# Token stage: small vector work moved to ScalarE, and the first convolution in three bf16 parts

## The chip, the cores and the metric

The kernel is one program on one core of a Trainium2 chip. The core has a matrix engine (TensorE, PE in the profile; its weight loads are PEld), VectorE (DVE), ScalarE (ACT), GpSimd (POOL) and SyncE (SP), which here issues the DMAs. Each engine takes its instructions in the order in which they stand in its own queue, and waits on semaphores for what other engines produce. The metric is the device time of one execution in microseconds (us).

## What is computed

Four layers follow one another on x of 64 images, 128 channels, 28 x 28 pixels, all in f32. Only the first and the last matter here.

Layer 0 is a residual block with quantised weights and activations:

```python
out = conv3x3(x, quant_weight(w1, 4))
out = quant_act(batchnorm(out, gamma1, beta1), 4)
out = conv3x3(out, quant_weight(w2 * (mask2 > 0.5), 4))
out = quant_act(batchnorm(out, gamma2, beta2) + x, 4)
```

`quant_weight` gives odd multiples of 1/15 between -1 and 1; the kernel keeps them as whole numbers from -15 to 15 and puts 1/15 into the scale of the batch norm. The input x of the first convolution is any f32 number.

Layer 1 is self-attention over the pixels of each image, layer 2 a Mamba scan over the pixels. Layer 3, the token stage, takes each pixel's 128 channels as a sequence of 8 tokens of 16 numbers and runs a Mamba over it, then normalises in four groups of channels and gates:

```python
xs = silu(causal_conv(xi)); dt, Bm, Cm = split(xs @ x_proj_w.T)
dt = softplus(dt @ dt_proj_w.T + dt_proj_b)
h = exp(dt * A) * h + dt * B * xs      # 8 tokens, 32 x 16 states a pixel
y = (sum over states of h * C) + xs * D
xr = (y * silu(z)) @ out_proj_w.T
gn = (xr - mu) * rsqrt(var + 1e-5)     # mean and variance of 32 channels and all pixels
out = x + silu(gn * gn_gamma + gn_beta)
```

## The kernel before

All tiles have 128 partitions. T is the 784 pixels of an image, and HT is half of that.

`conv_block` (L135) makes both convolutions. `quantised` (L147) prepares the weights: ScalarE takes the tanh, VectorE and one GpSimd reduction scale and round. The first weights q1 are f32 and the second, q2, are bf16. Then a loop over 32 pairs of images loads a pair into `xt` (128 x 2 x 784), and `conv3x3` (L116) makes each half image as nine matmuls, one per tap, that accumulate in PSUM; the source is a shifted window of the image and a tap at the border covers fewer columns. ScalarE copies the sum to `raw` (L182), VectorE takes the statistics (L184), and SyncE stores it. The pool of the large tiles holds three of each. After the batch norm (L101 to L112) a second loop reads `raw` back, quantises it with ScalarE (L196) and VectorE (L197, L199), and runs `conv3x3` on the bf16 tile `qa`.

`attention_and_mamba` (L491) records its operations in a plan of its own, which writes the order of the queues by its costs (all at L472 in the profile). The change does not touch it.

`token_mamba` (L1077) is a loop over 28 groups of 1792 pixels (14 columns of 128 pixels, G = 14), each in two halves of 16 of the 32 inner channels (dh = 0 and 1), each half in four blocks of four inner channels.

- `x_proj(k)` (L1179) makes B and C of a group: for each of seven pairs of pixel columns it loads rows, multiplies into a PSUM tile `two`, and copies that to `BC` (L1202), 512 columns that land in runs of two. It then makes the product of B and C summed over states (L1209 to L1216).
- `delta_u(k, dh)` (L1224) makes the step size and the input of a half: 16 `delta` scalings and four `u` copies on ScalarE, then softplus as max(v, 0) + log(1 + e) with e = exp(-abs(v)): two ScalarE steps, `w` = 1 + e on VectorE (L1254), two corrections on VectorE (L1255, L1256), the logarithm on ScalarE, and two GpSimd steps (L1259, L1260). L1263 makes `diag`.
- `exps(k, dh, i)` (L1266) is 64 exponentials of 98 columns on ScalarE that fill one `a` tile for one block. There are two such tiles.
- `block` (L1275) is the scan over the 8 tokens. GpSimd makes the inputs `db` (L1293, five tiles) and the first steps on `a` (L1304, L1306); VectorE multiplies, adds and reads out (L1305 to L1312) with the state h in PSUM; PE sums over the states with an identity (L1315, L1317, L1319) and so releases `a`; ScalarE copies the sum to `ysb`.
- `gate(k, dh, ysb)` (L1322) transposes back, multiplies (L1335, L1336) and, for dh = 1, projects (L1344) and copies the result to the image `xr` (L1354). When an image is full, `finish_image` (L1133) normalises and gates it: statistics on VectorE (L1137, L1139), the group mean by a matmul with `grp` (L1141), six one-column VectorE steps and two one-column ScalarE steps around a second group matmul (L1143 to L1152), two sign changes (L1153, L1154), three ScalarE steps for the gate's sigmoid, the scale and shift of the image on VectorE (L1162), and two GpSimd steps (L1164, L1165).

The results of `two`, the transposes and the group means take turns in one pool of three PSUM banks (`bank`). At the end of `token_mamba` generators mix the steps: while a half runs its blocks, it takes steps of the preceding half's `gate` (for dh = 1 they carry the images, so these run in the next half with dh = 0), of the next half's `delta_u`, and, in a dh = 0 half after its first block, of the next group's `x_proj`. From this program a scheduler with a simulated timeline then makes the order of each queue in the convolutions and the token stage. ScalarE operations of the token stage have the line of a helper, L228.

Of the kernel before, what the change touches and what calls it, by code (L numbers as in the profile page):

```python
# [16 lines left out]
F32 = mybir.dt.float32  # L17
BF16 = mybir.dt.bfloat16
# [7 lines left out]
C = 128  # L26
HW = 28
# [88 lines left out]
def conv3x3(nc, ps, w, src):  # L116

    img = src.rearrange("p (h w) -> p h w", w=HW)
    taps = [(0, 0)] + [(dy, dx) for dy in (-1, 0, 1) for dx in (-1, 0, 1) if (dy, dx) != (0, 0)]
    for half in range(2):  # L120
        acc = ps[:, half, :HT].rearrange("p (h w) -> p h w", w=HW)
        r0 = half * 14
        for i, (dy, dx) in enumerate(taps):
            lo, hi = max(r0, -dy), min(r0 + 14, HW - dy)
            a, b = max(0, -dx), min(HW, HW - dx)
            nc.tensor.matmul(  # L126
                acc[:, lo - r0 : hi - r0, a:b],
                lhsT=w[:, (dy + 1) * 3 + dx + 1, :],
                rhs=img[:, lo + dy : hi + dy, a + dx : b + dx],
                start=(i == 0),  # L130
                stop=(i == len(taps) - 1),
            )


def conv_block(tc, cpool, dram, x, w1t, w2t, m2t, v, eps):  # L135
# [6 lines left out]
    with ExitStack() as ctx:  # L142
# [4 lines left out]
        def quantised(name, src, mask, dtype):  # L147
# [19 lines left out]
            q = wp.tile([C, 9, C], dtype, name=f"q{name}")  # L167
# [3 lines left out]
        q1 = quantised("1", w1t, None, F32)  # L171
        q2 = quantised("2", w2t, m2t, BF16)

        st1 = wp.tile([C, NB * 2, 6], F32, name="st1")
        for g in range(NB // GRP):
            xt = big.tile([C, GRP, T], F32, name="xt")
            nc.sync.dma_start(xt, x[g * GRP : (g + 1) * GRP].rearrange("b c t -> c b t"))
            raw = big.tile([C, GRP, T], F32, name="raw")
            for k in range(GRP):
                acc = ps.tile([C, 2, 512], F32, name="acc")  # L180
                conv3x3(nc, acc, q1, xt[:, k, :])
                nc.scalar.copy(halves(raw[:, k, :]), acc[:, :, :HT])  # L182
                for h in range(2):
                    nc.vector.bn_stats(st1[:, (g * GRP + k) * 2 + h, :], raw[:, k, h * HT : (h + 1) * HT])  # L184
# [7 lines left out]
        for g in range(NB // GRP):  # L192
# [7 lines left out]
            for k in range(GRP):  # L200
                acc = ps.tile([C, 2, 512], F32, name="acc")
                conv3x3(nc, acc, q2, qa[:, k, :])
# [874 lines left out]
def token_mamba(tc, tables, x2d, utd, ztd, pk4, v, ident, eps, out, NB):  # L1077
# [17 lines left out]
    with ExitStack() as ctx:  # L1095
# [37 lines left out]
        def finish_image(b):  # L1133
# [8 lines left out]
            sm = p2.tile([C, 8], F32, name="sm", bufs=4)  # L1142
            nc.vector.tensor_copy(sm[:, 0:1], acc[:, 0:1])  # L1143
            nc.vector.tensor_sub(sm[:, 1:2], mv[:, 0:1], sm[:, 0:1])
            nc.vector.scalar_tensor_tensor(sm[:, 2:3], sm[:, 1:2], sm[:, 1:2], mv[:, 1:2], ALU.mult, ALU.add)
            acc2 = bank()
            nc.tensor.matmul(acc2[:, 0:1], lhsT=grp, rhs=sm[:, 2:3], start=True, stop=True)
            act(sm[:, 3:4], acc2[:, 0:1], AF.Ln, bias=eps)
            act(sm[:, 4:5], sm[:, 3:4], AF.Exp, scale=-0.5)
            nc.vector.tensor_mul(sm[:, 5:6], sm[:, 4:5], v("gn_gamma"))  # L1150
            nc.vector.tensor_mul(sm[:, 6:7], sm[:, 0:1], sm[:, 5:6])
            nc.vector.tensor_sub(sm[:, 7:8], v("gn_beta"), sm[:, 6:7])  # L1152
            nc.vector.tensor_scalar(sm[:, 0:1], sm[:, 5:6], -1.0, None, ALU.mult)  # L1153
            nc.vector.tensor_scalar(sm[:, 1:2], sm[:, 7:8], -1.0, None, ALU.mult)  # L1154
# [4 lines left out]
            act(e, xo, AF.Exp, bias=sm[:, 1:2], scale=sm[:, 0:1])  # L1159
            act(e, e, AF.Ln, bias=1.0)  # L1160
            act(e, e, AF.Exp, scale=-1.0)
            nc.vector.tensor_scalar(xo, xo, sm[:, 5:6], sm[:, 7:8], ALU.mult, ALU.add)  # L1162
# [16 lines left out]
        def x_proj(k):  # L1179
# [5 lines left out]
            for g, n in chunks:  # L1185
                uts = [load_rows(utd, k, dh, g, n) for dh in range(2)]
                for g2 in range(0, n, 2):
                    two = bank()
                    for j in range(2):
# [12 lines left out]
                    nc.vector.tensor_copy(  # L1202
                        BCf[:, :, g + g2 : g + g2 + 2], two.rearrange("p (c j) -> p c j", j=2)
                    )
# [19 lines left out]
        def delta_u(k, dh):  # L1224
# [29 lines left out]
            nc.vector.tensor_scalar(w_, e_, 1.0, None, ALU.add)  # L1254
# [244 lines left out]
```

## Time and profile before

| | us |
|---|---|
| median of 3 runs | 14449.58 (14403.58 to 14459.57) |
| profiled execution | 14456.75 |
| its span | 14454.9 |
| first convolution, first to last matmul | 18.6 to 744.6 |
| second convolution | 755.3 to about 940 |
| token stage, from its first preparation | 8085 |
| token stage, first to last block | 8144 to 14404, 6260 long |
| VectorE busy in these 6260 | 5781.8 |
| ScalarE | 4804.0 |
| GpSimd | 5165.3 |
| PE | 4363.2, mean clock 0.81 |

A group of instructions stands in the profile as line, engine, operation, output <- input, shapes and count; then busy time in us and the mean of one in ns; then the idle time of the engine just before these instructions and what ended most of it. A wait stands as engine, line and instruction that waits <- engine and line that it waited for, then total us, number of times, and the longest. Idle time of an engine that does not set the pace costs nothing.

### The profile page before, as it was taken

Reading aid. Unit: us, or ns where it says so; the run is one execution under the profiler, and the core shown is the slowest. Engines: PE = TensorE matmul, PEld = TensorE weight load, DVE = VectorE, ACT = ScalarE, POOL = GpSimd, SP = SyncE. Lnnn points to the kernel's source line nnn. Section 1 sums busy time; section 2 is a strip of 40 time slices with the busy share of each in tenths; the row PEclk is TensorE's granted clock in tenths of the full one; section 3 lists DMA queues with packets and bytes.
Section 4 is the critical chain, followed back from the end, with each engine's and each line's share of the span. In section 5 each row is a group of like instructions: output and inputs, shape, how many; then the busy total and the mean of one; then the engine's idle time right before and its main releaser. Section 6 shows DMA issues by size and latency. Waiting matters only on the chain. (4 is left out here: it accounts for less than half of the span.)

```text
span 14454.9 us, 181149 instructions
## 1 busy us (share of the span) xinstructions
PE 10855.2 (75%) x58370; PEld 7180.2 (50%) x58370; DVE 12706.4 (88%) x13524; ACT 10460.3 (72%) x25236; POOL 11391.7 (79%) x5304
## 2 busy tenths in 40 slices
PE   9987777777777777777776676776767767677676
PEld 5654444444444444444443455555555555555554
DVE  1048999999999999999999799999999999999998
ACT  0047777777777777777777677777777777777776
POOL 0007899889898888889889788888888887888887
PEclk9988888888888888888887787888878888888787
DMA  2243444444444444444444211111112111111111
GB/s 74 72 162 109 135 123 128 129 121 127 131 121 126 130 120 124 133 122 124 134 121 125 67 45 46 55 48 52 45 48 60 44 49 47 49 59 42 49 50 44
DMA packets 711515, 1297.64 MB, mean 90 GB/s; under 512 B 206624, under 2 KB 357536, under 8 KB 710560
## 3 DMA queue, kind: packets, MB, share of 16 engines
q1 hardware_dynamic: 710560, 1286.05, 29.8%
q8 instruction: 460, 7.54, 0.2%
q14 instruction: 495, 4.06, 0.1%
HBM read 954.72 MB, written 330.76 MB: 89 GB/s over the span
## 5 line engine op out<-in xcount | busy, mean ns | idle before, releaser
L228 ACT ACTIVATE a<-delta,A 128x98 f32<-128x98 f32 x14336 | 3906.2, 365 | 1123.2 <-PE y L1317 827.4
L472 POOL TENSOR_TENSOR h<-ur,Br 128x784 f32<-128x784 f32 x1920 | 4205.3, 2216 | 152.6 <-PE y L472 136.3
L1293 POOL TENSOR_TENSOR db<-u,BC 128x896 f32<-128x896 f32 x1568 | 3274.0, 2101 | 856.0 <-DVE h L1312 688.1
L1317 PE MATMUL y<-a,ident 128*128 128x280 f32 x7168 | 2089.5, 455 | 954.2 <-DVE a L1310 898.5
L472 DVE TENSOR_TENSOR_SCAN ah<-ah,h 128x392 f32<-128x392 f32 x2304 | 2303.1, 1000 | 60.8 <-ACT ah L472 50.3
L1317 PEld LDWEIGHTS y<-a,ident 128*128 128x128 f32 x7168 | 1557.7, 221 | 1512.4 <-POOL db L1293 729.1
L472 DVE TENSOR_TENSOR_SCAN h<-a,h 128x784 f32<-128x784 f32 x768 | 1915.0, 2498 | 112.7 <-ACT a L472 57.9
L472 ACT ACTIVATE ah<-dr,A 128x392 f32<-128x392 f32 x2304 | 1322.9, 587 | 612.8 <-DVE ah L472 592.4
L472 POOL TENSOR_TENSOR h<-h,Cr 128x784 f32<-128x784 f32 x640 | 1350.7, 2114 | 357.9 <-DVE h L472 347.5
L1308 DVE TENSOR_TENSOR h<-h,a 128x896 f32<-128x896 f32 x1344 | 1473.7, 1096 | 33.1
L472 DVE TENSOR_TENSOR h<-ah,Cr 128x392 f32<-128x392 f32 x2304 | 1302.5, 565 | 72.9
L472 PE MATMUL y<-h,fold 128*32 128x98 f32 (+1 forms) x12288 | 1024.0, 422 | 385.2 <-DVE h L472 357.2
L1312 DVE TENSOR_TENSOR h<-h,db 128x896 f32<-128x896 f32 x1120 | 1228.2, 1097 | 59.1 <-POOL db L1293 0.5
L472 POOL TENSOR_TENSOR xn<-s,sq 128x784 f32<-128x784 f32 x64 | 136.5, 2133 | 1183.6 <-ACT sq L472 1142.9
L472 PEld LDWEIGHTS bank<-vt,et 112*112 112x112 f32 x6272 | 905.4, 215 | 233.9 <-ACT et L472 90.6
L1310 DVE TENSOR_TENSOR a<-h,BC 128x896 f32<-128x896 f32 x896 | 974.1, 1087 | 21.4
L472 PE MATMUL bank<-vt,et 112*112 112x128 f32 x6272 | 981.6, 320 | 5.0 <-ACT et L472 2.3
L1319 PE MATMUL y<-late,ident 128*128 128x112 f32 x7168 | 848.0, 275 | 14.3 <-DVE late L1310 13.4
L1319 PEld LDWEIGHTS y<-late,ident 128*128 128x128 f32 x7168 | 838.5, 193 | 37.8 <-DVE late L1310 18.0
L472 PEld LDWEIGHTS y<-h,fold 128*32 128x32 f32 x12288 | 378.8, 121 | 909.7 <-DVE h L472 428.8
L472 ACT ACTIVATE a<-dr,A 128x784 f32<-128x784 f32 x768 | 716.8, 942 | 152.0 <-DVE h L472 150.4
L126 PE MATMUL acc<-xt,q 128*128 128x378 f32 (+3 forms) x2304 | 726.0, 478 | 18.6 <-DVE q L168 18.6
(213 smaller groups left out, 20969.2 us busy)
## 6 DMA issues: line engine op xcount, KB each, us to landing
Br<-bcd SPq DMA_DIRECT2D x1536, 98.0 KB, 2.4
Cr<-bcd SPq DMA_DIRECT2D x1536, 98.0 KB, 2.4
dr<-dud SPq DMA_DIRECT2D x1280, 98.0 KB, 2.4
ur<-dud SPq DMA_DIRECT2D x1280, 98.0 KB, 2.3
utd<-tok SPq DMA_DIRECT2D x128, 392.0 KB, 2.7
ztd<-tok SPq DMA_DIRECT2D x128, 392.0 KB, 3.7
rows<-utd SPq DMA_DIRECT2D x192, 256.0 KB, 2.8
xt<-in_x SPq DMA_DIRECT2D x32, 784.0 KB, 5.2
```

Of the source, the lines that this page charges most:

```text
L126: nc.tensor.matmul(acc[:, lo - r0 : hi - r0, a:b], lhsT=w[:, (dy + 1) * 3 + dx + 1, :], rhs=img[:, lo + dy : hi + dy, a + dx : b + dx], st ...
L228: ins = self.tc.nc.scalar.activation(*args, **kw)
L472: last = getattr(getattr(nc, engine), method)(*args, **kw)
L1293: nc.gpsimd.tensor_tensor(x, of_dg(du[:, t, ds, :]), BC[:, t, :NS, :].unsqueeze(1).broadcast_to([C, DB, NS, G]), ALU.mult)
L1308: nc.vector.tensor_tensor(h, h, flat(at(t)), ALU.mult)
L1310: nc.vector.tensor_tensor(by_d(dst), h_d, Cc(t), ALU.mult)
L1312: nc.vector.tensor_tensor(h, h, flat(inject(t)), ALU.add)
L1317: nc.tensor.matmul(y3[:, 1:6], lhsT=ident, rhs=a[:, 0:5, :, n, :], start=False, stop=False)
L1319: nc.tensor.matmul(y3[:, 6:8], lhsT=ident, rhs=late[:, :, :, n, :], start=False, stop=(n == NS - 1))
```

## The change

In the first convolution each f32 input pair is split into three bf16 tiles whose sum is the input: ScalarE casts it to the first part, VectorE subtracts that part, ScalarE casts the rest to the second part, and VectorE subtracts once more into the third. q1 becomes bf16, and each tap is three bf16 matmuls, one a part, into the same sum. The second convolution passes its one tile as a list of one.

In `finish_image` the one-column work goes to ScalarE in another form: Square with bias mv and scale -1 on the mean in PSUM, an Identity that adds the variance, and after Ln and Exp three Identities for gamma times rstd, mean times scale, and the shift. The scale and shift of the image becomes an Identity with two one-column operands, ahead of the gate's three steps, and the gate's first exponential loses its two operands. The mean stays in its PSUM tile `acc` until the fourth of these steps. In `x_proj` the copies of B and C, and in `delta_u` the step 1 + e, become ScalarE operations. The built program has the same number of activation table loads as before.

```diff
--- before.py
+++ after.py
@@ -113,9 +113,9 @@
     return s, b15
 
 
-def conv3x3(nc, ps, w, src):
-
-    img = src.rearrange("p (h w) -> p h w", w=HW)
+def conv3x3(nc, ps, w, parts):
+
+    imgs = [m.rearrange("p (h w) -> p h w", w=HW) for m in parts]
     taps = [(0, 0)] + [(dy, dx) for dy in (-1, 0, 1) for dx in (-1, 0, 1) if (dy, dx) != (0, 0)]
     for half in range(2):
         acc = ps[:, half, :HT].rearrange("p (h w) -> p h w", w=HW)
@@ -123,13 +123,14 @@
         for i, (dy, dx) in enumerate(taps):
             lo, hi = max(r0, -dy), min(r0 + 14, HW - dy)
             a, b = max(0, -dx), min(HW, HW - dx)
-            nc.tensor.matmul(
-                acc[:, lo - r0 : hi - r0, a:b],
-                lhsT=w[:, (dy + 1) * 3 + dx + 1, :],
-                rhs=img[:, lo + dy : hi + dy, a + dx : b + dx],
-                start=(i == 0),
-                stop=(i == len(taps) - 1),
-            )
+            for img in imgs:
+                nc.tensor.matmul(
+                    acc[:, lo - r0 : hi - r0, a:b],
+                    lhsT=w[:, (dy + 1) * 3 + dx + 1, :],
+                    rhs=img[:, lo + dy : hi + dy, a + dx : b + dx],
+                    start=(i == 0 and img is imgs[0]),
+                    stop=(i == len(taps) - 1 and img is imgs[-1]),
+                )
 
 
 def conv_block(tc, cpool, dram, x, w1t, w2t, m2t, v, eps):
@@ -144,7 +145,7 @@
         big = ctx.enter_context(tc.tile_pool(name="cv", bufs=3))
         ps = ctx.enter_context(tc.tile_pool(name="cvps", bufs=4, space=PSUM))
 
-        def quantised(name, src, mask, dtype):
+        def quantised(name, src, mask):
 
             w = wp.tile([C, 9 * C], F32, name="w", tag="wtmp", bufs=2)
             nc.sync.dma_start(w, src)
@@ -164,21 +165,27 @@
             nc.vector.tensor_scalar(t, t, r, 0.5, ALU.mult, ALU.add)
             nc.vector.tensor_scalar(t, t, 15.0, MAGIC, ALU.mult, ALU.add)
             nc.vector.tensor_scalar(t, t, MAGIC, 2.0, ALU.subtract, ALU.mult)
-            q = wp.tile([C, 9, C], dtype, name=f"q{name}")
+            q = wp.tile([C, 9, C], BF16, name=f"q{name}")
             nc.vector.tensor_scalar(q.rearrange("p k c -> p (k c)"), t, 15.0, None, ALU.subtract)
             return q
 
-        q1 = quantised("1", w1t, None, F32)
-        q2 = quantised("2", w2t, m2t, BF16)
+        q1 = quantised("1", w1t, None)
+        q2 = quantised("2", w2t, m2t)
 
         st1 = wp.tile([C, NB * 2, 6], F32, name="st1")
         for g in range(NB // GRP):
             xt = big.tile([C, GRP, T], F32, name="xt")
             nc.sync.dma_start(xt, x[g * GRP : (g + 1) * GRP].rearrange("b c t -> c b t"))
+
+            parts = [big.tile([C, GRP, T], BF16, name=f"part{i}") for i in range(3)]
+            nc.scalar.copy(parts[0], xt)
+            nc.vector.tensor_tensor(xt, xt, parts[0], ALU.subtract)
+            nc.scalar.copy(parts[1], xt)
+            nc.vector.tensor_tensor(parts[2], xt, parts[1], ALU.subtract)
             raw = big.tile([C, GRP, T], F32, name="raw")
             for k in range(GRP):
                 acc = ps.tile([C, 2, 512], F32, name="acc")
-                conv3x3(nc, acc, q1, xt[:, k, :])
+                conv3x3(nc, acc, q1, [m[:, k, :] for m in parts])
                 nc.scalar.copy(halves(raw[:, k, :]), acc[:, :, :HT])
                 for h in range(2):
                     nc.vector.bn_stats(st1[:, (g * GRP + k) * 2 + h, :], raw[:, k, h * HT : (h + 1) * HT])
@@ -199,7 +206,7 @@
             nc.vector.tensor_scalar(qa, act, MAGIC, None, ALU.subtract)
             for k in range(GRP):
                 acc = ps.tile([C, 2, 512], F32, name="acc")
-                conv3x3(nc, acc, q2, qa[:, k, :])
+                conv3x3(nc, acc, q2, [qa[:, k, :]])
                 raw = big.tile([C, T], F32, name="raw2")
                 nc.scalar.copy(halves(raw), acc[:, :, :HT])
                 for h in range(2):
@@ -1139,27 +1146,25 @@
             nc.vector.bn_aggr(mv, stats.rearrange("p n s -> p (n s)"))
             acc = bank()
             nc.tensor.matmul(acc[:, 0:1], lhsT=grp, rhs=mv[:, 0:1], start=True, stop=True)
-            sm = p2.tile([C, 8], F32, name="sm", bufs=4)
-            nc.vector.tensor_copy(sm[:, 0:1], acc[:, 0:1])
-            nc.vector.tensor_sub(sm[:, 1:2], mv[:, 0:1], sm[:, 0:1])
-            nc.vector.scalar_tensor_tensor(sm[:, 2:3], sm[:, 1:2], sm[:, 1:2], mv[:, 1:2], ALU.mult, ALU.add)
+
+            sm = p2.tile([C, 6], F32, name="sm", bufs=4)
+            act(sm[:, 0:1], acc[:, 0:1], AF.Square, bias=mv[:, 0:1], scale=-1.0)
+            act(sm[:, 1:2], sm[:, 0:1], AF.Identity, bias=mv[:, 1:2])
             acc2 = bank()
-            nc.tensor.matmul(acc2[:, 0:1], lhsT=grp, rhs=sm[:, 2:3], start=True, stop=True)
-            act(sm[:, 3:4], acc2[:, 0:1], AF.Ln, bias=eps)
-            act(sm[:, 4:5], sm[:, 3:4], AF.Exp, scale=-0.5)
-            nc.vector.tensor_mul(sm[:, 5:6], sm[:, 4:5], v("gn_gamma"))
-            nc.vector.tensor_mul(sm[:, 6:7], sm[:, 0:1], sm[:, 5:6])
-            nc.vector.tensor_sub(sm[:, 7:8], v("gn_beta"), sm[:, 6:7])
-            nc.vector.tensor_scalar(sm[:, 0:1], sm[:, 5:6], -1.0, None, ALU.mult)
-            nc.vector.tensor_scalar(sm[:, 1:2], sm[:, 7:8], -1.0, None, ALU.mult)
+            nc.tensor.matmul(acc2[:, 0:1], lhsT=grp, rhs=sm[:, 1:2], start=True, stop=True)
+            act(sm[:, 2:3], acc2[:, 0:1], AF.Ln, bias=eps)
+            act(sm[:, 2:3], sm[:, 2:3], AF.Exp, scale=-0.5)
+            act(sm[:, 3:4], v("gn_gamma"), AF.Identity, scale=sm[:, 2:3])
+            act(sm[:, 4:5], acc[:, 0:1], AF.Identity, scale=sm[:, 3:4])
+            act(sm[:, 5:6], sm[:, 4:5], AF.Identity, bias=v("gn_beta"), scale=-1.0)
             res = p1.tile([C, T], F32, name="res")
             nc.sync.dma_start(res, x2d[b])
 
             e = p1.tile([C, T], F32, name="gate")
-            act(e, xo, AF.Exp, bias=sm[:, 1:2], scale=sm[:, 0:1])
+            act(xo, xo, AF.Identity, bias=sm[:, 5:6], scale=sm[:, 3:4])
+            act(e, xo, AF.Exp, scale=-1.0)
             act(e, e, AF.Ln, bias=1.0)
             act(e, e, AF.Exp, scale=-1.0)
-            nc.vector.tensor_scalar(xo, xo, sm[:, 5:6], sm[:, 7:8], ALU.mult, ALU.add)
             yield
             nc.gpsimd.tensor_tensor(xo, xo, e, ALU.mult)
             nc.gpsimd.tensor_tensor(res, res, xo, ALU.add)
@@ -1199,9 +1204,7 @@
                                 dt_ps[:, :, g + g2 + j], lhsT=uts[dh][:, at], rhs=w("BDt", dh * NK, (dh + 1) * NK),
                                 start=(g + g2 + j == 0 and dh == 0), stop=(g + g2 + j == G - 1 and dh == 1),
                             )
-                    nc.vector.tensor_copy(
-                        BCf[:, :, g + g2 : g + g2 + 2], two.rearrange("p (c j) -> p c j", j=2)
-                    )
+                    act(BCf[:, :, g + g2 : g + g2 + 2], two.rearrange("p (c j) -> p c j", j=2), AF.Copy)
                 yield
             small = p2.tile([C, 2, NK, G], F32, name="small")
             nc.vector.tensor_copy(small[:, 0].rearrange("p t g -> p (t g)"), acc[:, : NK * G])
@@ -1251,7 +1254,7 @@
             act(e_, e_, AF.Exp, scale=-1.0)
             w1 = p1.tile([C, NK, ND, G], F32, name="w1")
             w_ = flat(w1)
-            nc.vector.tensor_scalar(w_, e_, 1.0, None, ALU.add)
+            act(w_, e_, AF.Identity, bias=1.0)
             nc.vector.scalar_tensor_tensor(e_, w_, 1.0, e_, ALU.subtract, ALU.subtract)
             nc.vector.scalar_tensor_tensor(v_, v_, 0.0, e_, ALU.max, ALU.subtract)
             yield
```

## The prediction

> **What bounds the kernel now.** I read the engine totals first, then stages by the table of windows, then the groups and waits of each stage the change touches. The program runs as first convolution (to 745 us), second convolution (to about 940), attention and first Mamba (to 8085), token stage (to the end).
>
> ```profile
> PE 10855.2 (75%) x58370; PEld 7180.2 (50%) x58370; DVE 12706.4 (88%) x13524; ACT 10460.3 (72%) x25236; POOL 11391.7 (79%) x5304
> ```
> ```profile
> 200.00:400.00 200.00, 200.00 (x639) 121.14 (x638) 18.66 (x36) 14.62 (x18) 0.00 (x0) 1.00 0.23 73
> 800.00:820.00 20.00, 20.00 (x126) 12.04 (x124) 13.71 (x21) 11.23 (x11) 0.00 (x0) 1.00 0.85 275
> ```
>
> In each row stand start:end, length, then PE, PEld, DVE, ACT, POOL, then PE's clock and the DMA. Both convolutions are PE alone: busy throughout at clock 1.00, ScalarE and VectorE under 10% in the first. The first convolution issues f32 operands and the second bf16, on the same shapes.
>
> The token stage is different. I cut it into its 53 half-groups at each start of the `diag` multiply (L1263). Two examples, the half with dh=1 first, then one with dh=0 (it also copies B and C and finishes the images):
>
> ```profile
> 11359.70:11452.44 92.74, 58.63 (x266) 45.27 (x266) 83.25 (x83) 68.31 (x222) 83.74 (x40) 0.74 0.22 69
> ...
> 11452.44:11573.83 121.39, 92.50 (x421) 74.14 (x422) 112.76 (x113) 89.77 (x309) 88.82 (x44) 0.79 0.13 36
> ```
>
> Means: dh=0 half 121.5 us (VectorE 112.7, ScalarE 93.4, GpSimd 96.2), dh=1 half 103.0 us (94.7, 79.4, 88.8). VectorE is 92% busy in both, so it sets the pace, and it idles little:
>
> ```profile
> DVE h L1305 <- POOL a L1304: 151.7, 62, 6.2
> DVE BC L1202 <- PE bank L1192: 43.0, 39, 3.7
> ```
>
> What leaves VectorE, and what ScalarE has free:
>
> ```profile
> L1202 DVE COPY BC<-bank 128x512 f32<-128x512 f32 x196 | 133.7, 683 | 62.9 <-PE bank L1192 60.6 <-DMA ztd<-tok 1.4
> ...
> L1254 DVE TENSOR_SCALAR w<-e 128x1792 f32<-128x1792 f32 x56 | 129.1, 2305 | 15.2 <-ACT e L228 15.2
> ...
> L1162 DVE TENSOR_SCALAR xr<-xr,sm 128x784 f32<-128x784 f32 x64 | 78.2, 1221 | 3.5 <-ACT gate L228 3.3
> ...
> L1150 DVE TENSOR_TENSOR sm<-sm,vec 128x1 f32<-128x1 f32 x64 | 43.0, 672 | 16.8 <-ACT sm L228 16.8
> ```
> ```profile
> ACT a L228 <- PE y L1317: 827.4, 137, 19.9
> ACT u L228 <- PE bank L1239: 182.8, 76, 8.8
> ```
>
> The last two say that ScalarE, 77% busy here, mostly waits for a free `a` buffer. That wait is slack only while the exponentials still end before their block begins.
>
> **What the Trainium skill says.** "TensorE: Matmul & The Clock Gate", Back-to-back issue gap, gives N/2.4 + 2.5 ns for a warm matmul. A tap has 373.6 columns on average, so 158 ns; the trace agrees, with 5.84 us for 36 taps in the second convolution (copies L204 at 800.72 and 806.56), 162 ns. "FP8 and Floating Point Precision" says that true FP32 takes 4 passes; the trace agrees, 726 us over 1152 taps, 630 ns or 3.9 times 162. "SBUF — State Buffer", Who interferes with whom, says that a VectorE instruction with two SBUF inputs, or in a 2-port mode, and GpSimd shut each other out for a whole instruction. The trace agrees: the one-column multiply L1150 takes 141 ns at its shortest and 2039 at its longest, about one GpSimd instruction. "ScalarE: Activation LUTs", What ACT_TABLE_LOAD costs, prices an ACTIVATE at 186 ns + 0.833 ns an element, and 93 ns per pointer operand; the trace has 845 for 784 columns without pointers and 1036 with two.
>
> **Convolution.** Removed: 1152 f32 taps, 726 us (18.6 to 744.6). Added: 3456 bf16 matmuls at 162 ns, 560 us. Per pair of images PE takes 17.5 us; beside it lie ScalarE's two casts (1.69 us each, row L196) and two copies (0.81), 5.0 us, and VectorE's two subtractions (estimate 1.75 each, from 1.09 for 896 columns) and four statistics (0.56), 5.7 us. In the built order the casts run three pairs ahead, so they are hidden; uncovered, their chain of 7 us a pair would cost 32 x 7 = 224 us. SyncE's loads wait for VectorE's last subtraction in place of PE, which is earlier. At the start they are not hidden: VectorE's queue has four subtractions, q1 and a scaling before the first third part is ready, 17.5 + 4 x 1.75 + 1.9 = 26.3 us against 18.6, in which PE does about 0.8 us: 7 us. Sum 560 + 7 - 726 = -159. The clock of a stretch of bf16 this long is not shown: 185 us held 1.00, so I take 1.00; at 0.81 (token stage) it would be 691 + 7 - 726 = -28.
>
> **Attention.** Its instructions stand in the same order in both programs: 0.
>
> **Token stage, VectorE.** Per image eight one-column operations go (the five two-input ones 35.6 to 43.0 us each in total, the other three 9.1 to 9.5: 228.1), and the scale and shift (78.2). With the BC copies (133.7) and 1+e (129.1) that is 569.1. Neighbours overlap by about 0.08 us, 828 times, so it frees 503 us: 2.2 per dh=1 half (its 1+e), 15.8 per dh=0 half. The waits in front of these rows, 62.9 + 16.8 + 15.2 + 3.5 + 2.4 = 101 us, leave VectorE too, but move to ScalarE's queue.
>
> **Token stage, ScalarE.** BC copies 196 x 0.605 (the 512-column PSUM copy to `u`) = 119; were its two-element runs slow to write, up to 1.03, +83; I take 0.605. 1+e 56 x 1.69 = 95. Scale and shift 64 x 1.036 = 66, while the first exponential loses its pointers, 64 x -0.19 = -12. Five one-column operations 64 x 5 x 0.245 (between 0.192 and 0.248) = 78. Sum 346, less 0.095 overlap on 196 copies: 327, or 1.7 per dh=1 half and 10.0 per dh=0 half. The added waits: Square waits for the group-mean matmul, and Ln for the second one, which in the built order stands behind matmuls L1317 that wait for VectorE; behind them on ScalarE are the next `delta` scalings and 64 exponentials, for which GpSimd's L1304 and so VectorE's L1305 wait. `acc` now stays in one of three PSUM banks until the fourth ScalarE step. These waits are not in the trace: from below 0, for ScalarE would often have waited there for `a`; from above 5.6 us a dh=0 half (its idle beyond that for `a` is 1456 - 827 = 629 us, 22 a group; if 14 of it stays in that half, 117.4 instead of 111.8). GpSimd gains up to 103 us of shared port (64 x 0.67 + 56 x 1.08); I count nothing.
>
> **Sum.** dh=0 half: VectorE 112.7 - 15.8 = 96.9, GpSimd 96, ScalarE 93.4 + 10.0 = 103.4. ScalarE is late next. With the idle share that VectorE has now (7.5%) 103.4/0.925 = 111.8. dh=1 half: VectorE 92.5/0.92 = 100.5, ScalarE 81. A group takes 212.3 for 224.5; 28 x 12.2 = 342, say -340. The profiled execution took 14456.75 us (span 14454.9): -159 - 340 gives 13958. It is 7 above the median, so 13950.
>
> **Rivals.** (1) VectorE gets all of it back, waits too: -159 - 604, 13687. For it: 92% busy; against it: three engines would have to run above 91% in queues that wait for each other. (2) ScalarE's in-order waits bind in the dh=0 half: 117.4 + 100.5, group -6.6, -185: 14106. For it: L1304 already starts on exponentials just ended (22 times, 76.6 us). (3) The clock falls in the bf16 stretch: -28 - 340, 14082. (4) Slower: the image chain holds its bank and the exponentials behind it. Nothing is lost while a stall is under 7.8 us per image: 2.29 images a group then bring the dh=0 half from 111.8 to 129.6, where the token stage gives back the convolution's 159. At 12 us per image, the half is 139 and the stage 28 x 15 = 420 longer: 14710. Against it: the longest wait of ScalarE for a mean (L1147) is 16.6 us but all such waits are 32 us in 64 images. That the change does not act is excluded by the built order: the instructions are there.
>
> **Chances.** Forecast 0.55 (own range 13850 to 14060), (1) 0.14, (2) 0.22, (3) 0.06, (4) 0.03. The range 13770 to 14150 leaves out half of (1), the tail of (2), (4) and the tails of the forecast, 0.18. It covers slow BC copies (+83). Within 0.5%, about what a measurement of this kernel can tell from no change, only a bad case of (2): 0.02. Slower 0.03, faster 0.95.
>
> **What would show it.** The last conv1 matmul at 585 to 590 us, at 162 ns a tap and clock 1.00; VectorE without `sm` rows and 83 to 88% busy in the token stage; ScalarE 85 to 88%, its wait on L1317 below 500 us; dh=0 halves near 112 us, dh=1 near 100. A longer wait of L1305 on L1304 than 151.7 us shows ScalarE late. The prediction is wrong if conv1 is not PE-bound after, or if dh=1 halves move by more than 5 us.

## The result, and the profile after

| | before | after |
|---|---|---|
| median, us | 14450.95 (14403.58 to 14459.57) | 14040.17 (14023.01 to 14058.70) |
| profiled execution, us | 14456.75 | 14058.70 |
| first convolution, first matmul to end | 18.6 to 744.6 | 18.5 to 586.0 |
| second convolution and attention, to 8085 before | 7340 | 7326 |
| token stage, first to last GpSimd step on `a` (L1304, after L1307) | 8160.4 to 14380.6 = 6220.2 | 7982.6 to 13983.2 = 6000.6 |

The ratio is 0.9722 with an interval of 0.9697 to 0.9748, 411 us less. In the two profiled executions it is 398: 159 in the convolution, 220 between the two outer steps of the token stage, 14 in between, and 5 in the token stage's start and end. The 14 are no gain of the change: the stretch in between has the same code in all kernels here, and it took 7320 to 7343 us in the 13 of them that have the new convolution. In the kernel after, most lines of the token stage stand three further down (L1304 is L1307, L1317 is L1320), the group matmuls L1141 and L1147 are L1148 and L1154, the matmul of B and C (L1192) is L1197, and the ScalarE helper is L235.

The engine totals of the page after, then the chain of work that ended last, first of before, then of after:

```profile
PE 10623.3 (76%) x59522; PEld 7022.5 (50%) x59522; DVE 12350.4 (88%) x12760; ACT 10874.1 (77%) x25936; POOL 11465.4 (82%) x5304
```
```profile
DVE 22%; PE 8%; POOL 6%; ACT 3%; issue 3%; DMA 1%; SPq 0%; DVEq 0%; POOLq 0%; ACTq 0%
```
```profile
DVE 12%; ACT 11%; PE 10%; POOL 7%; issue 2%; DMA 1%; SPq 0%; POOLq 0%; DVEq 0%; ACTq 0%
```

The chain passed mostly through VectorE; now VectorE, ScalarE and PE have nearly equal shares of it. The exponentials alone hold 9% of the span in it, for 3% before.

The convolution after, as windows (start:end, length, PE, PEld, DVE, ACT, POOL, clock, DMA), the second row being the token stage:

```profile
18.50:586.00 567.50, 564.54 (x3456) 338.11 (x3456) 177.94 (x194) 139.03 (x124) 0.00 (x0) 1.00 0.25 90
...
7982.60:13983.20 6000.60, 4310.31 (x20670) 3418.17 (x20671) 5288.10 (x4829) 5091.44 (x16651) 5215.93 (x2459) 0.81 0.17 51
```

PE is busy for 564.5 of 567.5 us at full clock, 163 ns for each of 3456 matmuls; after the first 400 they start every 162 ns. The token stage before, in the same form:

```profile
8160.40:14380.60 6220.20, 4337.16 (x20641) 3440.33 (x20642) 5744.73 (x5611) 4787.09 (x16033) 5138.32 (x2460) 0.81 0.17 49
```

VectorE lost 456.6 us of busy time but the stage only 219.6: VectorE is idle 237 us more (475.5 before, 712.5 after). The waits in the token stage after say where (engine and line that waits <- whom, total us, times, longest; the copies of the first group, which stand ahead of the stage, are left out):

```profile
ACT a L235 <- PE y L1320: 454.2, 102, 14.2
...
DVE h L1308 <- POOL a L1307: 381.0, 108, 13.5
...
ACT BC L235 <- PE bank L1197: 193.2, 73, 9.2
...
POOL a L1307 <- issue: 101.5, 29, 10.2
```

VectorE's wait for GpSimd's first step on `a` was 151.7 us and is 381.0: 229 of the 237. I call this wait (L1308 for L1307, under other numbers in the experiments) VectorE's lateness. The starts and ends in the trace divide it in two. In 38 of the 108 waits, 179 us together, GpSimd starts within 0.3 us of the block's last exponential, so there the exponentials are late; before the change these were 3 of 62 waits and 3 us. In the others, 202 us after and 149 before, the exponentials had ended earlier and GpSimd was still busy with its own steps, mostly `db`. A stretch of the first kind in the timeline after (start, duration, then the idle time of that engine ahead of it):

```profile
11053.97 0.62 ACT L235 ACTIVATE BC<-bank 128x512 f32<-128x512 f32 x1 [6.89 <-PE bank L1197]
...
11102.50 0.32 ACT L235 ACTIVATE sm<-sm,mv 128x1 f32<-128x1 f32 x1
11102.69 2.28 ACT L235 ACTIVATE a<-delta,A 128x98 f32<-128x98 f32 x8
11105.10 2.08 POOL L1307 TENSOR_TENSOR a<-a,db 128x896 f32<-128x896 f32 x1 [4.53 <-issue]
...
11107.22 1.10 DVE L1308 TENSOR_TENSOR h<-a,db 128x896 f32<-128x896 f32 x1 [6.41 <-POOL a L1307]
```

Ahead of a copy of B and C ScalarE stands idle for 6.89 us, since the copy's matmul is late. From 11057.72 on it has no idle time any more: in 47 us it makes the 128 exponentials of two blocks and, between them, three more copies, 16 `delta` scalings and steps of three images. The last eight exponentials end at 11104.97, GpSimd, 4.53 us idle, starts 0.13 later, and VectorE, 6.41 us idle, when GpSimd has ended. So waiting and work both stand ahead of these late exponentials.

The moved operations by shape, after (count, then busy us and mean ns, then idle ahead of them), with the two image steps that wait for a group matmul, Square and Ln, at the end:

```profile
L235 ACT ACTIVATE BC<-bank 128x512 f32<-128x512 f32 x196 | 119.7, 613 | 206.9 <-PE bank L1197 204.8 <-DMA ztd<-tok 2.1
...
L235 ACT ACTIVATE w<-e 128x1792 f32<-128x1792 f32 x56 | 95.9, 1713 | 1.4 <-ACT sm L235 0.5
...
L235 ACT ACTIVATE xr<-xr,sm 128x784 f32<-128x784 f32 x64 | 68.2, 1065 | 0.0
...
L235 ACT ACTIVATE sm<-bank,eps 128x1 f32<-128x1 f32 x64 | 17.1, 267 | 3.0 <-PE bank L1154 2.8
L235 ACT ACTIVATE sm<-bank,mv 128x1 f32<-128x1 f32 x64 | 16.7, 261 | 14.9 <-PE bank L1148 14.9
```

The copies cost 120 us of work and bring 205 us of idle time of their own. On VectorE the same copies had waited 62.9. Square and Ln wait for 18 us in all.

### The profile page after: what moved, and what is told of

It reads as the page before. It is cut to its first block, busy times and chain, and to the rows that moved or that the text cites. A ratio compares the mean times of both kernels' runs of the same rounds, so it can differ in the third digit from the quotient of the medians.

```text
span 14056.9 us, 183402 instructions
## 1 busy us (share of the span) xinstructions
PE 10623.3 (76%) x59522; PEld 7022.5 (50%) x59522; DVE 12350.4 (88%) x12760; ACT 10874.1 (77%) x25936; POOL 11465.4 (82%) x5304
## 5 line engine op out<-in xcount | busy, mean ns | idle before, releaser
L235 ACT ACTIVATE a<-delta,A 128x98 f32<-128x98 f32 x14336 | 3966.8, 380 | 512.7 <-PE y L1320 454.2
L1296 POOL TENSOR_TENSOR db<-u,BC 128x896 f32<-128x896 f32 x1568 | 3337.2, 2144 | 548.4 <-DVE h L1315 531.0
L1320 PE MATMUL y<-a,ident 128*128 128x280 f32 x7168 | 2083.5, 452 | 815.3 <-DVE a L1313 811.5
L1320 PEld LDWEIGHTS y<-a,ident 128*128 128x128 f32 x7168 | 1549.1, 220 | 1371.4 <-POOL db L1296 582.9
L1308 DVE TENSOR_TENSOR h<-a,db 128x896 f32<-128x896 f32 x224 | 394.1, 1759 | 388.4 <-POOL a L1307 381.0
```

The source lines that it names most:

```text
L235: ins = self.tc.nc.scalar.activation(*args, **kw)
L1296: nc.gpsimd.tensor_tensor(x, of_dg(du[:, t, ds, :]), BC[:, t, :NS, :].unsqueeze(1).broadcast_to([C, DB, NS, G]), ALU.mult)
L1308: nc.vector.tensor_tensor(h, flat(at(1)), flat(inject(1)), ALU.add)
L1320: nc.tensor.matmul(y3[:, 1:6], lhsT=ident, rhs=a[:, 0:5, :, n, :], start=False, stop=False)
```

## The experiments

All kernels below have the new convolution. The token stage's part of the change consists of three pieces: the image work (one-column steps, scale and shift), the 1 + e, and the copies of B and C. My first theory was that ScalarE's in-order queue is late next, so that a piece on ScalarE is worth less the more ScalarE already holds. The rivals were that the convolution gave less than it seemed, that one piece is simply a loss, and that VectorE's own work is the limit still. All combinations of the three pieces were run, so that the pieces can be priced alone and together; then five runs looked for the mechanism. Where expectations give theories letters, the first ones are the theory and the rivals of this paragraph; C, D, E, G and H are put in words beside their runs.

### conv_only: no piece of the token stage

```diff
-            act(sm[:, 0:1], acc[:, 0:1], AF.Square, bias=mv[:, 0:1], scale=-1.0)
...
+            nc.vector.tensor_copy(sm[:, 0:1], acc[:, 0:1])
...
-                    act(BCf[:, :, g + g2 : g + g2 + 2], two.rearrange("p (c j) -> p c j", j=2), AF.Copy)
+                    nc.vector.tensor_copy(BCf[:, :, g + g2 : g + g2 + 2], two.rearrange("p (c j) -> p c j", j=2))
...
-            act(w_, e_, AF.Identity, bias=1.0)
+            nc.vector.tensor_scalar(w_, e_, 1.0, None, ALU.add)
```

> The kernel before with the first convolution of the change alone. Every theory: the first convolution ends near 586 us as in the changed kernel, and the rest is unchanged, 14450 - 159 = about 14290. The token stage (first to last GpSimd step on a) should take 6220 us as before, with VectorE's wait for that step at about 150 us. If instead the convolution gives more or less than 159, the division of the gain between the two stages is wrong.

Measured: 14290.08 us, ratio 0.9898 (0.9879 to 0.9916). Its token stage took 6229.6 us between the outer steps (6220.2 before), and VectorE's lateness is that of before:

```profile
DVE h L1312 <- POOL a L1311: 152.8, 63, 5.0
```

So the convolution gives its 142 to 159 us, and nothing of it is lost later.

### bc_dve: the copies of B and C back on VectorE

```diff
-                    act(BCf[:, :, g + g2 : g + g2 + 2], two.rearrange("p (c j) -> p c j", j=2), AF.Copy)
+                    nc.vector.tensor_copy(BCf[:, :, g + g2 : g + g2 + 2], two.rearrange("p (c j) -> p c j", j=2))
```

> The changed kernel with the copies of B and C back on VectorE. Theory A, exponentials come late because ScalarE's queue stands behind copies that wait for PE (193 us of wait, 120 us of work): ScalarE is free of 313 us, VectorE's wait for GpSimd's first step on a falls from 381 us to 230 or less and pays for the 134 us of copies and their wait of about 45 us: 14040, within 40. Theory B, VectorE's own load sets the time: 180 us slower, 14220. Theory C, the group means hold a PSUM bank: no change of VectorE's wait, 14150 to 14220.

Measured: 14014.94 us (14010.53 to 14019.97), ratio 0.9707 (0.9688 to 0.9725). VectorE gets 134 us of work back and the kernel is not slower. This is what the first theory expected. Its lateness falls by 160, the late exponentials in it from 179 to 85:

```profile
ACT a L235 <- PE y L1322: 454.2, 86, 16.3
...
DVE h L1310 <- POOL a L1309: 221.5, 83, 7.2
```

### fin_dve: the image work back on VectorE

```diff
-            act(sm[:, 0:1], acc[:, 0:1], AF.Square, bias=mv[:, 0:1], scale=-1.0)
...
+            nc.vector.tensor_copy(sm[:, 0:1], acc[:, 0:1])
...
-            act(xo, xo, AF.Identity, bias=sm[:, 5:6], scale=sm[:, 3:4])
...
+            nc.vector.tensor_scalar(xo, xo, sm[:, 5:6], sm[:, 7:8], ALU.mult, ALU.add)
```

> The changed kernel with the one-column work and the scale and shift of the images back on VectorE. VectorE gets about 250 us of work back, ScalarE loses 148 us of work and 18 us of wait. Theory A: VectorE's wait for GpSimd's first step on a falls by some 100 us, so 150 slower, 14190. Theory B: 250 slower, 14290. Theory C, the means hold a PSUM bank through ScalarE's steps and PE's later matmuls wait for it: ScalarE's waits for B and C copies and u fall from 364 us to under 200, and the kernel is within 40 of 14040 or faster.

Measured: 14097.07 us, ratio 0.9764 (0.9742 to 0.9786). By the medians it is 57 us slower, where the first theory had 150 and the rival 250. Lateness is 161.1, so nearly that of before, while the copies wait as long as in the kernel after (193.2):

```profile
ACT BC L235 <- PE bank L1199: 189.8, 83, 8.1
...
DVE h L1310 <- POOL a L1309: 161.1, 73, 11.9
```

So the waiting of the copies alone makes VectorE hardly later.

### e_dve: 1 + e back on VectorE

```diff
-            act(w_, e_, AF.Identity, bias=1.0)
+            nc.vector.tensor_scalar(w_, e_, 1.0, None, ALU.add)
```

> The changed kernel with 1 + e back on VectorE. VectorE gets back 125 us of work[...]; ScalarE loses 96 us, in both halves. Theory A: the wait for GpSimd's first step on a falls by 50 to 100 us and the kernel is 30 to 70 slower, 14070 to 14110. Theory B: 125 slower, 14165. Theory C: as B.

Measured: 14148.46 us (14114.61 to 14153.53), ratio 0.9794 (0.9773 to 0.9815). Lateness 288.8. The 108 us lie near the rival's 125 and outside the theory's 30 to 70.

### fin_only: of the pieces, the image work alone is moved

```diff
-                    act(BCf[:, :, g + g2 : g + g2 + 2], two.rearrange("p (c j) -> p c j", j=2), AF.Copy)
+                    nc.vector.tensor_copy(BCf[:, :, g + g2 : g + g2 + 2], two.rearrange("p (c j) -> p c j", j=2))
...
-            act(w_, e_, AF.Identity, bias=1.0)
+            nc.vector.tensor_scalar(w_, e_, 1.0, None, ALU.add)
```

> The kernel before with the first convolution of the change and the image work of the change on ScalarE; 1 + e and the copies of B and C stay on VectorE. It frees about 306 us of VectorE's queue and 23 us of its waits, and asks 133 us of ScalarE, which has 790 us of wait for a free a tile. Theory A (ScalarE's lateness takes back most of the rest): ScalarE is not late yet, so most of it is kept: 14290 - 250 = 14040, VectorE's wait for GpSimd's first step on a below 200 us. Theory B (each part gives the same wherever it stands): the 57 us that undoing it cost, 14233.

Measured: 14113.79 us, ratio 0.9781 (0.9765 to 0.9798). Lateness 230.9. Theory A (14040, lateness below 200) and theory B (14233) both miss; the time lies between them.

### e_only: 1 + e alone is moved

```diff
-            act(sm[:, 0:1], acc[:, 0:1], AF.Square, bias=mv[:, 0:1], scale=-1.0)
...
+            nc.vector.tensor_copy(sm[:, 0:1], acc[:, 0:1])
...
-                    act(BCf[:, :, g + g2 : g + g2 + 2], two.rearrange("p (c j) -> p c j", j=2), AF.Copy)
+                    nc.vector.tensor_copy(BCf[:, :, g + g2 : g + g2 + 2], two.rearrange("p (c j) -> p c j", j=2))
```

> The kernel before with the first convolution of the change and 1 + e on ScalarE, nothing else moved. Theory A: 129 us less for VectorE, which ScalarE has free: 14290 - 120 = 14170. Theory B: the 108 us that undoing it cost, 14182. The two hardly differ here; the run is needed for the sum of the parts.

Measured: 14179.72 us, ratio 0.9824 (0.9809 to 0.9838). Lateness 144.4.

### bc_only: the copies alone are moved

```diff
-            act(sm[:, 0:1], acc[:, 0:1], AF.Square, bias=mv[:, 0:1], scale=-1.0)
...
+            nc.vector.tensor_copy(sm[:, 0:1], acc[:, 0:1])
...
-            act(w_, e_, AF.Identity, bias=1.0)
+            nc.vector.tensor_scalar(w_, e_, 1.0, None, ALU.add)
```

> The kernel before with the first convolution of the change and the copies of B and C on ScalarE, nothing else moved. VectorE loses 134 us of work and 45 us of wait. Theory A as to work (ScalarE is too full only once the other parts are there too): 14290 - 130 = 14160. Theory A as to waits (the copies hold up the exponentials behind them whatever else runs there): ScalarE waits about 190 us for PE at the copies, VectorE's wait for GpSimd's first step on a rises from 153 us to 250 or more, and the time stays within 40 of 14290. Theory B: 25 slower than 14290, as undoing it made the whole kernel 25 faster.

Measured: 14178.84 us, ratio 0.9826 (0.9811 to 0.9841). This is near what the theory expected of the work, and not what it expected of the waits: the copies wait here as well, and yet VectorE's lateness is below the 152.8 of conv_only:

```profile
ACT BC L235 <- PE bank L1199: 145.8, 73, 6.7
...
DVE h L1310 <- POOL a L1309: 120.5, 52, 6.1
```

### The eight combinations together

The gain stands against conv_only: difference of the ratios times 14432, the median of before beside these runs. One ratio's interval is about 20 to 40 us to each side. Behind the lateness stands the part of it in which GpSimd starts within 0.3 us of the last exponential. The halves are cut at `diag` as in the prediction, without the first three and the last of the stage (26 of each kind).

| on ScalarE | kernel | ratio | gain, us | lateness (late exponentials), us | half dh=0, dh=1, us | ScalarE busy in each |
|---|---|---|---|---|---|---|
| none | conv_only | 0.9898 | 0 | 153 (7) | 121.2, 102.9 | 92.9, 79.3 |
| 1 + e | e_only | 0.9824 | 107 | 144 (9) | 116.8, 101.8 | 93.6, 81.8 |
| copies | bc_only | 0.9826 | 104 | 121 (18) | 116.4, 103.5 | 92.4, 84.0 |
| image | fin_only | 0.9781 | 169 | 231 (81) | 111.1, 105.7 | 85.1, 90.6 |
| copies, 1 + e | fin_dve | 0.9764 | 193 | 161 (41) | 110.0, 105.8 | 91.0, 88.1 |
| image, 1 + e | bc_dve | 0.9707 | 276 | 222 (85) | 107.3, 105.9 | 85.7, 93.3 |
| image, copies | e_dve | 0.9794 | 150 | 289 (86) | 113.7, 105.8 | 86.9, 92.8 |
| all | after | 0.9722 | 254 | 381 (179) | 109.7, 105.5 | 87.8, 95.4 |

Image and 1 + e add up exactly (169 + 107 = 276), copies and 1 + e nearly (211 for 193). Image and copies do not: 273 would be their sum and 150 came, 123 short, and all three are short by 126 (380 for 254). With its four intervals the shortfall of 123 is uncertain by about 50. The same pair can be taken a second time, with 1 + e on ScalarE in all four kernels: 276 + 193 - 107 = 362 would be the sum and 254 came, 108 short. The other two pairs, taken both ways too, differ from their sums by 18 us or less. So one pair of pieces clashes, and the rival that a piece is a loss by itself falls: the copies alone gain 104 us. The first theory falls in its general form: 1 + e gains 107 us alone and 104 on top of the other two, though ScalarE holds more then. On top of the other two pieces the copies give nothing (22 us worse, where the intervals overlap).

The clash does not show in one wait. In after the late exponentials are 179 us, more than the 85 of bc_dve and the 41 of fin_dve would lead one to expect. In e_dve they are 86, hardly more than with the image work alone (81); there it is VectorE's waits for results of PE that are long: 224 us in the token stage, for 139 in fin_only, 108 in bc_only and 167 in conv_only.

### bc_twice: each copy made twice on ScalarE

```diff
                     act(BCf[:, :, g + g2 : g + g2 + 2], two.rearrange("p (c j) -> p c j", j=2), AF.Copy)
+                    act(BCf[:, :, g + g2 : g + g2 + 2], two.rearrange("p (c j) -> p c j", j=2), AF.Copy)
```

> The changed kernel with each copy of B and C made twice on ScalarE, the second over the first: 119 us more of work on ScalarE and no new wait for another engine. If the work of the copies is what makes the exponentials late, it costs as much again as the first copies did: undoing them gained 25 while it gave VectorE about 180 us back, so up to 200 us, 14140 to 14240. If their wait for PE in ScalarE's queue is what costs, the second copies cost little: within 40 of 14040.

Measured: 14075.12 us, ratio 0.9750 (0.9736 to 0.9765), 40 us above after by the ratios, uncertain by about as much, for 117 us more in the row of the copies (237.1 for 119.7). Lateness is 286.6, and the copies wait 164.6. The work of the second copies is mostly covered, far from the 200 us that the first theory allowed, so ScalarE's busy time alone does not make the first ones worthless. That their waiting does is not shown by this: in fin_dve they wait as long, and little is lost.

### early: the mean leaves its PSUM bank at once

The theory (C) was that `acc`, held until the fourth ScalarE step, leaves two banks to the copies' matmuls.

```diff
-            act(sm[:, 0:1], acc[:, 0:1], AF.Square, bias=mv[:, 0:1], scale=-1.0)
+            act(sm[:, 6:7], acc[:, 0:1], AF.Copy)
+            act(sm[:, 0:1], sm[:, 6:7], AF.Square, bias=mv[:, 0:1], scale=-1.0)
...
-            act(sm[:, 4:5], acc[:, 0:1], AF.Identity, scale=sm[:, 3:4])
+            act(sm[:, 4:5], sm[:, 6:7], AF.Identity, scale=sm[:, 3:4])
```

> The changed kernel with the group mean copied out of PSUM first (one more one-column ScalarE step per image, 16 us in all), and the later steps reading that copy. The image work and the copies of B and C gave 145 us less together than apart. Theory C (the mean holds one of three PSUM banks through four ScalarE steps, so the matmuls of B and C, and the copies behind them, wait for it): 60 to 110 us come back, 13930 to 13980, and ScalarE's wait at the copies falls from 193 us to below 120. Theory D (ScalarE and PE wait for each other's queue at the second mean matmul, 77.8 us): no change, 14040 to 14060. Theory E (ScalarE's one-image steps are too large for that half): no change.

Measured: 14110.84 us, ratio 0.9774 (0.9760 to 0.9789), 75 above after. The copies wait as long as before the edit (193.2):

```profile
ACT BC L235 <- PE bank L1198: 194.5, 70, 8.1
```

The hold of the bank is not what they wait for. The theory falls. Lateness fell to 288.5 and the kernel became slower all the same; that 64 steps of a quarter of a microsecond, 16 us, do this is not explained. With both intervals the 75 us are uncertain by about 45.

### head_dve: the first two one-column steps on VectorE

The theory (D) was a mutual wait: the second group matmul on PE waits for ScalarE's first two steps, and the copies' matmuls stand behind it.

```diff
-            act(sm[:, 0:1], acc[:, 0:1], AF.Square, bias=mv[:, 0:1], scale=-1.0)
-            act(sm[:, 1:2], sm[:, 0:1], AF.Identity, bias=mv[:, 1:2])
+            nc.vector.tensor_sub(sm[:, 0:1], mv[:, 0:1], acc[:, 0:1])
+            nc.vector.scalar_tensor_tensor(sm[:, 1:2], sm[:, 0:1], sm[:, 0:1], mv[:, 1:2], ALU.mult, ALU.add)
```

> The changed kernel with the two first one-column steps (squared difference of the mean, plus variance) on VectorE as a subtraction and a multiply-add; the bank of the mean is held as in the changed kernel. VectorE gets 46 us of work back. Theory D (PE's second mean matmul waits for a ScalarE step queued behind exponentials, and the matmuls of B and C behind it make the copies wait): PE's wait at that matmul moves to VectorE and the copies' 193 us fall to below 120; 40 to 100 us faster, 13940 to 14000. Theory C or E: 20 to 50 us slower, 14060 to 14090.

Measured: 14058.99 us, ratio 0.9740 (0.9724 to 0.9756), 26 above after. Lateness falls to 277.3, and the late exponentials in it from 179 to 28, the most of all edits, but the copies wait no less:

```profile
ACT BC L235 <- PE bank L1197: 205.3, 75, 7.7
```

The theory is not supported: the exponentials are hardly late any more, and the kernel is no faster. In the waits that remain GpSimd is busy with its own steps.

### scale_dve: the scale and shift of the image on VectorE

The theory (E) was that the long steps, not the short ones, push the exponentials back.

```diff
-            act(xo, xo, AF.Identity, bias=sm[:, 5:6], scale=sm[:, 3:4])
+            nc.vector.tensor_scalar(xo, xo, sm[:, 3:4], sm[:, 5:6], ALU.mult, ALU.add)
```

> The changed kernel with the scale and shift of the image (784 columns) back on VectorE, the one-column work still on ScalarE. VectorE gets 78 us of work[...] back, ScalarE loses 68 us in the half with the images. Theory E (the large steps fill ScalarE in that half): VectorE's wait for GpSimd's first step on a falls by 60 us or more from 381 and the time stays within 20 of 14040 or falls. Theories C and D: 40 to 80 us slower, 14080 to 14120.

Measured: 14103.74 us, ratio 0.9773 (0.9758 to 0.9787), 74 above after; lateness 279.8, wait of the copies 195.3. Lateness fell as the theory had it, the time rose as its rivals had it. The step is worth having on ScalarE, late or not.

### xproj_early: the next group's B and C begun one block earlier

By blocks, the lateness of after lies mostly in the fourth block of dh=0 (83 us over all groups), and in the first and third of dh=1 (94 and 88); without the copies it is 9, 87 and 32 (bc_dve), without the image work 2, 29 and 18 (fin_dve). In the fourth block e_dve has 51 us, and the kernels that lack the image work or the copies on ScalarE have at most 9. The theory (G) was that copies and image work meet in the fourth block; its rival (H) that the wait only moves.

```diff
-                if dh == 0 and i > 0:
+                if dh == 0:
                     take(group_next, 2)
```

> The changed kernel with the steps that make B and C of the next group begun one block earlier (in the first block of the dh=0 half), so that in ScalarE's queue all their copies stand ahead of the image steps; the work is the same. Where the trace of the changed kernel has VectorE late by 83 us in the fourth block, after copies that wait 131 us in the third, it had 7 us with the copies on VectorE. Theory G (copies and image steps meet in the same two blocks, where ScalarE has no slack left): the lateness of the fourth block falls below 25 us, of the next one below 70, and most of the 145 us that the two cost together come back: 13930 to 13990. Theory H (copies that wait for PE hold up the exponentials wherever they stand): their wait only moves to the first block, beside the wait for u, VectorE's lateness stays above 300 us in all and the time within 40 of 14040.

Measured: 14113.21 us, ratio 0.9771 (0.9754 to 0.9787), 71 above after. The fourth block's lateness went from 83 to 4 us, so the place was right. But the copies now wait mostly in the first two blocks, longer in all, and VectorE waits for the projection's results on PE twice as long as in after (54.0):

```profile
DVE h L1308 <- POOL a L1307: 258.9, 107, 11.2
ACT BC L235 <- PE bank L1197: 257.3, 100, 7.6
...
DVE xr L1357 <- PE bank L1347: 110.1, 61, 5.3
```

So G falls. H was right in that the wait only moves, but missed both numbers: it had the lateness above 300 us and the time within 40 of 14040.

## Why the prediction was right in the main and too large in its gain

**The convolution** was right in every term that counts: end at 586.0 us, clock 1.00, 162 ns from matmul to matmul, 7 us lost at the start. -159 forecast, -158.5 in the trace. The casts took 1.50 us for 1.69, the subtractions 1.79 for 1.75.

**The token stage** was to give 340 us and gave 220 between its outer steps. The mechanism was in part the one forecast, ScalarE late next: lateness above 151.7 was the sign named, and it is 381.0. Between those steps VectorE's busy time fell by 457 us where I counted 503 for the whole stage (three images, two of the 1 + e and 14 of the 196 copies lie ahead of the first step or behind the last one, about half of the difference), and its idle time rose by 237. The forecast, which let 340 of 503 us reach the end, had allowed 163. These 46 and 74 us are the 120 missing. Of the 237 us of idle time 176 are late exponentials (3 before, 179 after) and 53 the rest of the lateness. The experiments give the same sum another way: by the ratios, the three pieces moved alone gain 380 us, more than the 340, and together 126 less. The forecast had no term of its own for pieces that cost each other something.

**The step that failed** is the sum for the half with dh=1, "VectorE 92.5/0.92 = 100.5, ScalarE 81". It kept VectorE's idle share of before, 8%, and it put all but 1.7 us of ScalarE's new work into the half with dh=0, where its code is. Two neighbouring halves of after, dh=1 and then dh=0, both near the means of the table:

```profile
13227.75:13333.85 106.10, 72.09 (x354) 57.88 (x354) 90.08 (x77) 95.92 (x313) 93.32 (x44) 0.84 0.21 63
13333.85:13444.18 110.33, 86.72 (x398) 67.58 (x398) 99.89 (x100) 85.21 (x279) 92.88 (x45) 0.81 0.14 39
```

The fourth and fifth numbers with a count are ScalarE and GpSimd. ScalarE's work in a group, 87.8 + 95.4 = 183.2 us, is what I had (103.4 + 81 = 184.4), and VectorE's too (189.5 for 189.4). But by this cut ScalarE's stands in the other half: with dh=1 ScalarE is the fullest engine, above VectorE, whose idle share there is 15%, and that half is 105.5 us, 5.0 longer than forecast, while dh=0 ends at 109.7, 2.1 shorter than forecast, with ScalarE busy for 80% of it and not for 92.5. Where the cut is made matters: at GpSimd's first step on `a` (L1304, L1307) the halves went from 116.2 and 108.2 to 110.5 and 105.4, and ScalarE's work in them rose by 4.3 and 6.5. By either cut the group lost 8 to 9 us where 12.2 was forecast, and dh=1 got far more than its 1.7.

**Of the signs**, VectorE 88.1% and ScalarE 84.9% busy (5288.1 and 5091.4 of 6000.6) lie just outside what I named, 83 to 88 and 85 to 88. The wait for `a` is 454.2, below 500 as forecast. The half with dh=1, whose move by more than 5 us was to show the prediction wrong, moved by 2.5, but it became longer where it was to become shorter by as much. The dearest single term, copies at 0.605 us, was right (0.613): their runs of two were not slow to write. The waits of Square and Ln, which I had named as the risk, came to 18 us, and those of the copies, for which I had no number of their own, to 205. "The Trainium skill", page "ScalarE: Activation LUTs", What ACT_TABLE_LOAD costs, has 186 ns + 0.833 ns an element: 1679 ns for 1 + e, where the run has 1713. Durations were thus not what failed.

**Of the rivals**, (1), all of VectorE's time given back, is excluded. (2), in-order waits on ScalarE, is nearer to what came: its token stage was to give 185, the forecast's 340, and 220 came; but it put the loss into the half with dh=0, which is where the forecast held. (3) did not occur, nor (4). That the time still lies in the forecast's own range, near its upper end, is owed to the convolution, which was exact; 14 us of the profiled gain are luck, from the stretch in which nothing was changed.

**What stays open** is why image work and copies clash. It is shown that they do, by 123 and 108 us in two comparisons. That the copies' waiting does it is not shown: they wait 189.8 us in fin_dve, where little is lost. Nor is it shown that late exponentials are the cause, and not only where the loss appears in after. Each of the five edits made the lateness shorter, and none made the kernel faster (the last column is VectorE's waits for results of PE in the token stage):

| kernel | above after by the ratios, us | lateness (late exponentials), us | waits for PE, us |
|---|---|---|---|
| after | 0 | 381 (179) | 162 |
| bc_twice | 40 | 287 (146) | 202 |
| early | 75 | 289 (97) | 218 |
| head_dve | 26 | 277 (28) | 205 |
| scale_dve | 74 | 280 (74) | 199 |
| xproj_early | 71 | 259 (83) | 235 |

Each build has its own order of the queues, and one edit of 16 us of work moved the time by 75, so a small gain can't be put down to one wait. A third `a` tile, which would test directly how much lead the exponentials lack, wasn't tried.

The lowest ratio is that of bc_dve, the change with the copies left on VectorE: 0.9707 against 0.9722. The two intervals overlap, so it is not shown to be faster; it has 196 operations fewer on ScalarE.

## What to carry to other kernels

When work leaves the engine that sets the pace, ask not only whether the next engine has room for it, but what each moved instruction waits for and which instructions queue behind it: 120 us of copies brought 205 us of idle time to an engine that was feeding the next block. Price pieces of a change alone and together: here each helped by 104 to 169 us alone, and two of them took 123 back when joined. A long wait is not yet a price: five edits made the wait that had grown most shorter, and other waits and work took its place. Work in a queue need not stay in the half of the loop in which it is written, so a sum by halves needs the order of the moved instructions, not the place of their code.

## What was not expected of the hardware

- PE held clock 1.00 over 567 us of bf16 matmuls with 3 us of gaps, three times as long as the 185 us that the kernel before shows.
- GpSimd's scan steps gained nothing when 828 operations left VectorE: `db` went from 2101 to 2144 ns, the second step on `a` from 2288 to 2366. Only its two image steps became shorter, from 2.08 to 1.93 us.
- ScalarE's instructions became a little longer: exponentials 365 to 380 ns, the gate's steps 845 to 880; the one-column steps took 261 to 316 ns where I had 245. A fuller queue alone is not the reason: with each copy made twice (bc_twice) the exponentials took 375.
- VectorE's first step of a block took 1.56 us in the mean where it had waited for GpSimd and 1.95 where it had not; over all blocks its mean went from 2059 to 1759 ns, 67 us in all. So in after, VectorE got back a part of what it waited. In early, with a lateness of 288.5, the mean is 2021, so this does not follow from the wait alone.
